# An attention block in fp32: group statistics of later images moved to VectorE, v's bias moved, last division sent through DRAM

## The chip, the cores and the metric

The kernel runs on one core of one Trainium2 chip. A core has a matrix engine (TensorE; in the profile PE for the matmuls and PEld for the weight loads), VectorE (DVE), ScalarE (ACT), GpSimd (POOL) and SyncE (SP). SP, ACT and POOL issue the DMAs here. The metric is the device time of one execution in microseconds (us). TensorE writes only to PSUM, which VectorE and ScalarE empty.

## What is computed

The input is 16 images of 512 channels by 32x32 positions (1024). Per image: group norm with 8 groups of 64 channels, a product with a 1536x512 matrix to q, k and v, attention with 4 heads of 128 channels over the 1024 positions, a product with a 512x512 matrix, and the residual. All in fp32.

```python
xg = x.reshape(b, NUM_GROUPS, -1)
mu = jnp.mean(xg, axis=-1, keepdims=True)
var = jnp.var(xg, axis=-1, keepdims=True)
xn = ((xg - mu) * jax.lax.rsqrt(var + EPS)).reshape(b, c, h, w)
xn = xn * norm_gamma[:, None, None] + norm_beta[:, None, None]
qkv = jnp.einsum('oc,bchw->bohw', qkv_w, xn) + qkv_b[:, None, None]
q, k, v = jnp.split(qkv, 3, axis=1)
...
attn = jax.nn.softmax(jnp.einsum('bhnd,bhmd->bhnm', q, k) * scale, axis=-1)
out = jnp.einsum('bhnm,bhmd->bhnd', attn, v)
out = out.transpose(0, 1, 3, 2).reshape(b, c, h, w)
out = jnp.einsum('oc,bchw->bohw', proj_w, out) + proj_b[:, None, None]
return x + out
```

## The kernel before

**Tiles.** A tile has 128 partitions. An image is 4 tiles x of 128 channels by 1024 positions; a PSUM bank holds 512 fp32 columns. An fp32 matmul appears in the profile as two instructions.

**The fast path.** The softmax is computed without subtracting a maximum. At the end one number tells whether all sums of exponentials and their inverses were in bounds (spans, LIMIT); only if not, a general path runs, which the diff touches in one line and which runs in no measurement here.

**The loop.** The main loop goes through 16 images x 4 heads x 8 steps, where a step is a block of 128 key positions. In a step `scores` (L843) makes s for both halves of the queries (L846), ScalarE takes the exponential to p (L852), VectorE adds p to the running sum tot (L858 and L860, one 128x1024 instruction a step), and one step later `weighted_sum` (L937) adds v times p to po (L942). After a head's last step ScalarE copies po to o (L949). In the next head's steps `denominators` (L864) sums tot over its partitions with transposes and a reduction on VectorE and takes the inverse r; `spread_inverse` (L887) writes r to DRAM as one row and reads the row back on all 128 partitions (rinv); `divide` (L951) multiplies o by rinv.

**What fills the steps.** Between these matmuls stand the projections, cut into units by `plan_head` (L1089). They use Strassen's seven products, for q and k, v and the output projection two levels deep (`two_levels`, L523, matmuls of 256 columns at L606; sums of the moving blocks at L574: tiles qk_t, v_t, pp_t). Their results leave PSUM at L486 and L628 (ScalarE) and L630 (VectorE), are combined at L679 and finished at L714 (q and k), L768 (v) and L826, L829 (output). While head 0 of image b runs, PE also makes q and k of b's second pair; with head 1 the output projection of b - 1; with head 2 q and k of b + 1, with head 3 v of b + 1. Weight sums are made once, during image 0 (`group_weights`, L392: tiles w, w_v, w_proj, with st_a as raw blocks), stored to DRAM (L443) and loaded again for each image through SP (L408), into buffers that two groups take in turn.

**Order.** The program is written in one order, and a scheduler orders each engine's instructions by their estimated readiness and priority. `tc.high_priority(URGENT)` brings an instruction ahead, `tc.issue_after(i)` keeps it behind instruction i, `keep_in_program_order` pins it. Each engine then runs its instructions in that fixed order, and an instruction that waits holds up what stands behind it on its engine.

**Group statistics.** During head 1 of image b, ScalarE sums each tile of image b + 1 and its squared distances (`stats_chunk`, L258, into mv: mean and variance of each channel). `stats_group` (L272) then makes 10 small steps (`Norm.group_steps`, L61): the channel means go through a matmul with a block matrix avg (pm, L83), VectorE takes the differences, their squares and adds the variances (L82 to L87), a second matmul averages these (pv, L88), VectorE adds EPS (ve, L89), GpSimd takes the power of -0.5 (rstd, L90), and sc and sh follow (L76, L100, L102). They are cut into three parts, behind tot's sums of steps 2, 3 and 4. Then ScalarE normalises x (L109). Image 0 has its own opening (`open_image`) with the same steps.

**v's bias.** Because the weights of the attention add up to 1, v's bias can be added later. `bias_of_v` (L959) multiplies it by the projection's weights, 16 small matmuls in image 0's head 1 (pb, L965), and adds the result to the projection's bias.

**The end.** The last head has no following head to hide its division. `last_division` (L898) sums tot over its partitions on PE: 8 small matmuls with a column of ones (l_last, L904), an inverse on VectorE, products with an identity, and two 512-column matmuls with a square of ones (rows, L922), which put the inverses on all partitions; VectorE multiplies o by them (L927). `last_projection` (L1023) is a one-level Strassen product (lx, ly, lz, L1031); its parts 1 and 5 need nothing of head 3, the others do. `last_span` (L930) adds the last head's check, a second matmul pair of most (L1078).

## Time and profile before

| what | value |
|---|---|
| median of 3 runs | 3172.76 us (3171.57 to 3177.14) |
| the profiled execution's span | 3170.7 us |
| VectorE busy / ScalarE / GpSimd | 83% / 45% / 16% of the span |
| granted TensorE clock | 1.00 throughout |
| one image in the steady part | about 195.8 us |
| pm (L83), 17 pairs; pv (L88), 17 pairs | first at 8 us, last at 2857 and 2864 us |
| pb (L965) | 32 instructions, 121.7 to 137.1 us |
| mean wait-free small VectorE instruction (L82 to L102) | 0.15 to 0.16 us |
| rstd (L90) on GpSimd, 128x4, median | 2.03 us |
| row to DRAM (L891), time to landing | 1.3 to 5.0 us, median 1.7 |
| rinv from DRAM (L896), 512 KB, time to landing | 3.3 to 11.1 us, median 4.9 |

Times of instructions are counted from the start of the span. A row of the order of time gives the start, the busy time, the engine, the line and operation, the tile written and the tiles read, sizes, and the number of instructions merged into the row; in brackets the idle time of the engine just before and what ended it. Matmuls overlap: their cost on PE is read from the distance between starts, not from their length.

### The profile page before, as it was taken

To read this page: it belongs to the slowest core of one execution; us is meant where nothing else is said; L and a number is where in the kernel's file an instruction comes from. 1 tells how busy PE (TensorE), PEld (TensorE's weight loads), DVE (VectorE), ACT (ScalarE), POOL (GpSimd) and SP (SyncE) were. 2 spreads that over 40 slices of the span, in tenths; PEclk is the share of its full clock that TensorE was granted. 3 is DMA by queue.
4 is the path that set the end of the run, shared out by engine and by line. 5 is a ranking of instruction groups with operands and counts; after the bars stand their busy time and mean duration, and the time that the engine had idled before them with its cause. 6 is when DMAs were issued, how large, how long until landed. Compare 5 with 4: busy or idle time off the path is not lost.

```text
span 3170.7 us, 34267 instructions
## 1 busy us (share of the span) xinstructions
PE 3159.9 (100%) x10524; PEld 2190.7 (69%) x10524; DVE 2633.6 (83%) x4639; ACT 1439.7 (45%) x2712; POOL 517.7 (16%) x898
## 2 busy tenths in 40 slices
PE   9999999999999999999999999999999999999999
PEld 7566676677766676777767767677676776766764
DVE  9878879788897888878788787987879978788784
ACT  3535435354353543545435453453534545344342
POOL 0011221111211112211122111222012221122200
PEclk9999999999999999999999999999999999999999
DMA  5554554555545455454554545555455564555531
GB/s 177 185 190 154 188 172 154 171 153 192 171 164 162 153 185 175 167 167 145 191 172 162 171 145 187 171 172 172 144 175 169 176 189 134 174 162 186 179 116 41
DMA packets 210333, 524.32 MB, mean 165 GB/s; under 512 B 32096, under 2 KB 65376, under 8 KB 210144
## 3 DMA queue, kind: packets, MB, share of 16 engines
q1 hardware_dynamic: 132896, 282.12, 28.8%
q0 software_dynamic: 64000, 204.54, 19.2%
q10 hardware_dynamic: 13248, 35.39, 3.5%
q8 instruction: 87, 1.43, 0.2%
q14 instruction: 102, 0.84, 0.1%
HBM read 388.77 MB, written 133.17 MB: 165 GB/s over the span
## 4 chain that ended last, share of the span: by engine, by line
PE 96%; DVE 3%; DMA 0%; issue 0%; POOL 0%; SPq 0%; ACT 0%; DVEq 0%; POOLq 0%
PE po L942 27%; PE s L846 27%; PE qk_x L606 12%; PE qk_y L606 9%; PE pp_x L606 6%; PE v_x L606 6%; PE pp_y L606 4%; PE v_y L606 4%; PE lx L1031 0%; DVE qk_t L574 0%; PE ly L1031 0%; PE warm L1153 0%; DVE tot L860 0%; DVE qk L714 0%; DVE qk_r L630 0%
## 5 line engine op out<-in xcount | busy, mean ns | idle before, releaser
L942 PE MATMUL po<-p,v 128*128 128x512 f32 x2048 | 1049.5, 594 | 0.7 <-ACT p L852 0.7
L846 PE MATMUL s<-qk,qk 128*128 128x512 f32 x2048 | 1047.4, 593 | 0.3 <-DVE qk L714 0.3
L852 ACT ACTIVATE p<-s 128x512 f32<-128x512 f32 x1024 | 610.9, 597 | 961.0 <-PE s L846 957.2
L942 PEld LDWEIGHTS po<-p,v 128*128 128x128 f32 x2048 | 603.6, 302 | 322.7 <-issue 214.5
L860 DVE TENSOR_TENSOR tot<-tot,p 128x1024 f32<-128x1024 f32 x385 | 469.0, 1218 | 158.4 <-ACT p L852 156.3
L846 PEld LDWEIGHTS s<-qk,qk 128*128 128x128 f32 x2048 | 387.7, 190 | 88.6 <-issue 29.9
L606 PEld LDWEIGHTS qk_x<-qk_t,w 128*128 128x128 f32 x1344 | 251.8, 190 | 166.1 <-issue 75.3
L606 PE MATMUL qk_x<-qk_t,w 128*128 128x256 f32 x1344 | 356.3, 382 | 0.1
L486 ACT COPY qk_u<-qk_x 128x512 f32<-128x512 f32 (+1 forms) x256 | 136.3, 533 | 229.2 <-PE qk_x L606 229.2
L779 POOL DMA_DIRECT2D vd<-vu x120 | 66.7, 557 | 899.8 <-DVE vu L771 897.9
L630 DVE TENSOR_TENSOR qk_r<-qk_y,qk_u 128x512 f32<-128x512 f32 (+1 forms) x256 | 157.7, 616 | 34.7 <-ACT qk_u L486 21.6
L580 POOL DMA_DIRECT2D kept_t<-qk_t x240 | 129.4, 540 | 278.4 <-DVE qk_t L574 211.9
L606 PEld LDWEIGHTS pp_x<-pp_t,w_proj 128*128 128x128 f32 x630 | 117.2, 190 | 74.7 <-issue 32.3
L784 POOL DMA_DIRECT2D v<-vd x240 | 140.6, 593 | 167.1 <-DMA vd<-vu 70.3
L630 DVE TENSOR_TENSOR v_r<-v_y,v_u 128x512 f32<-128x512 f32 (+1 forms) x120 | 76.0, 633 | 110.6 <-ACT v_u L486 80.3
L606 PE MATMUL pp_x<-pp_t,w_proj 128*128 128x256 f32 x630 | 167.8, 383 | 0.0
L606 PE MATMUL v_x<-v_t,w_v 128*128 128x256 f32 x630 | 166.6, 381 | 0.0
L830 POOL DMA_DIRECT2D out_y<-y x120 | 66.0, 550 | 604.2 <-DVE y L829 602.4
L606 PEld LDWEIGHTS v_x<-v_t,w_v 128*128 128x128 f32 x630 | 118.4, 190 | 55.3 <-issue 19.1
L606 PE MATMUL qk_y<-x,w 128*128 128x256 f32 x512 | 142.1, 379 | 0.0
L714 DVE SCALAR_TENSOR_TENSOR qk<-qk_r,qkb_sb,qk_r 128x512 f32<-128x512 f32 x192 | 137.5, 743 | 1.6
L486 ACT COPY v_u<-v_x 128x512 f32<-128x512 f32 (+1 forms) x124 | 66.3, 535 | 157.1 <-PE v_x L606 130.3
(217 smaller groups left out, 4487.2 us busy)
## 6 DMA issues: line engine op xcount, KB each, us to landing
w<-kept SPq DMA_DIRECT2D x90, 512.0 KB, 3.7
kept_t<-qk_t POOLq DMA_DIRECT2D x180, 256.0 KB, 3.3
v_t<-kept_t SPq DMA_DIRECT2D x180, 256.0 KB, 2.9
w<-kept SPq DMA_DIRECT2D x90, 384.0 KB, 3.4
rinv<-row ACTq DMA_DIRECT2D x63, 512.0 KB, 4.9
x<-in_x POOLq DMA_DIRECT2D x60, 512.0 KB, 4.6
vd<-vu POOLq DMA_DIRECT2D x120, 256.0 KB, 3.1
v<-vd POOLq DMA_DIRECT2D x240, 128.0 KB, 4.2
```

The source lines that it names most:

```text
L486: nc.scalar.copy(t[n][:, :width], t["x"][:, :width])
L580: nc.gpsimd.dma_start(t, to)
L606: nc.tensor.matmul(acc[:, ts(i, Q)], have["w"][t][:, i, slot, :], inner(i, bn), start=(first and i == 0), stop=True, skip_group_check=True,)
L630: nc.vector.tensor_add(dst, view(a), view(c))
L714: nc.vector.scalar_tensor_tensor(st[b, h][:, ts(half, HALF)], a, qkb_sb[:, i : i + 1], c, ALU.add, ALU.add)
L779: nc.gpsimd.dma_start(rows[which][ts(h, P), :], u)
L784: nc.gpsimd.dma_start(vs[b, pair][ts(q, BLK), half].rearrange("m h (k i) j -> m (h k) (i j)", k=n), rows[which].rearrange("(k m) (q e) -> ...
L830: nc.gpsimd.dma_start(out[b, ts(o, P), ts(half, HALF)], t)
L846: nc.tensor.matmul(sc, ks[b, h][:, ts(j, P)], qs[b, h][:, ts(half, HALF)], start=True, stop=True)
L852: exps[s] = nc.scalar.activation(ps[s][:, ts(half, HALF)], sc, AF.Exp, scale=SCALE)
L860: added[b, h, j] = nc.vector.tensor_add(tot[b, h][:, i], tot[b, h][:, i], ps[s][:, i])
L942: nc.tensor.matmul(po[b, h][:, i], v_block(b, h, j), ps[s][:, i], start=(j == 0), stop=(j == NB - 1),)
```

## The change

- The statistics of images 1 to 15 make no matmul. ScalarE writes means and sums of squared distances into one table of 128 x 2 x 32, of which 4 columns each are used and the rest is zero. VectorE transposes the table by blocks of 32x32, copies each block of 32 partitions beside its partner, so that the 64 channels of a group stand in one row with a count of 1024 each, and aggregates them with the instruction that combines means and spreads (bn_aggr). It adds EPS; GpSimd takes the power on one column; VectorE transposes mean and power back and makes sc and sh. All of it is one unit, behind tot's sum of step 3, urgent. Image 0 keeps its old way.
- v's bias is added to v where v is finished (images 1 to 15, with the addition at L768 as a three-operand instruction), and to image 0's attention output on ScalarE after its division. `bias_of_v` is gone.
- The last head's denominators go the way of the others: `denominators` on VectorE, urgent, r to DRAM through SP, and the row back on all partitions in two halves through SP and ACT; VectorE multiplies each half. ones_sq, the identity, the small matmuls and `last_span` are gone; spans has one more column. In `last_projection` the first chunks of products 2 and 6, which need nothing of head 3, come ahead of their second chunks.

```diff
@@ -256,41 +256,54 @@
     norm = Norm(nc, gn, ps_a, avg, neghalf, gamma_sb, beta_sb, NCC, N, "y")
 
     def stats_chunk(b, c):
-        if c == 0:
-            mvs[b] = gn.tile([P, NCC, 2], F32, tag="mv", name=f"mv_{b}")
-
+        mean, spread_ = (
+            (mvs[b][:, c, 0:1], mvs[b][:, c, 1:2]) if b == 0
+            else (table[:, 0, c : c + 1], table[:, 1, c : c + 1])
+        )
         junk = lpool.tile([P, N], F32, tag="tt", name=f"junk_{b}_{c}")
         sums = gn.tile([P, 3], F32, tag="st", name=f"sums_{b}_{c}")
         nc.scalar.activation(junk, xs[b, c], AF.Identity, accum_out=sums[:, 0:1])
-        nc.scalar.mul(mvs[b][:, c, 0:1], sums[:, 0:1], 1.0 / N)
+        nc.scalar.mul(mean, sums[:, 0:1], 1.0 / N)
         nc.scalar.mul(sums[:, 1:2], sums[:, 0:1], -1.0 / N)
         nc.scalar.activation(
-            junk, xs[b, c], AF.Square, bias=sums[:, 1:2], accum_out=sums[:, 2:3]
+            junk, xs[b, c], AF.Square, bias=sums[:, 1:2],
+            accum_out=sums[:, 2:3] if b == 0 else spread_,
         )
-        nc.scalar.mul(mvs[b][:, c, 1:2], sums[:, 2:3], 1.0 / N)
+        if b == 0:
+            nc.scalar.mul(spread_, sums[:, 2:3], 1.0 / N)
 
     def stats_group(b):
 
 
-        g = []
-
-        def part(n, first, last):
-            if not g:
-                g.extend(norm.group_steps(mvs[b]))
-            with tc.issue_after(added[b - 1, 1, n].ins), tc.high_priority(URGENT):
-                for step in g[first:last]:
-                    step()
-
-        def scale():
-            n = 4 if b > 1 else 3
-            part(n, 9, 10)
-            with tc.issue_after(added[b - 1, 1, n].ins), tc.high_priority(URGENT):
-                mu, sc = norm.result
-                sh = norm.shift(mu, sc)
+        v = nc.vector
+        quads = P // BLK
+        k = slice(0, NCC)
+
+        def steps():
+            t = lpool.tile([P, N], F32, tag="tt", name=f"groups_{b}")
+            rows = t[:, : 6 * BLK].rearrange("p (s j) -> p s j", s=3)
+            both = t[:, 6 * BLK : 6 * BLK + 2]
+            ve = t[:, 6 * BLK + 2 : 6 * BLK + 3]
+            back = t[:, 8 * BLK : 10 * BLK].rearrange("p (s j) -> p s j", s=2)
+            v.memset(rows[:, 0, :], float(N))
+            v.transpose(rows[:, 1:3, :BLK], table)
+            for q in range(quads):
+                v.tensor_copy(rows[ts(q, BLK), 1:3, BLK:], rows[ts(q ^ 1, BLK), 1:3, :BLK])
+            v.bn_aggr(both, rows.rearrange("p s j -> p j s"))
+            v.tensor_scalar_add(ve, both[:, 1:2], EPS)
+            nc.gpsimd.tensor_tensor(both[:, 1:2], ve, neghalf[:, 0:1], ALU.pow)
+            v.transpose(back, both.unsqueeze(2).to_broadcast([P, 2, BLK]))
+            sc = gn.tile([P, NCC], F32, tag="sc", name="sc")
+            v.tensor_mul(sc, back[:, 1, k], gamma_sb)
+            sh = norm.shift(back[:, 0, k], sc)
             for c in range(NCC):
                 scaled[b, c] = sc, sh, c
 
-        return [lambda: part(2, 0, 6), lambda: part(3, 6, 9), scale]
+        def all_():
+            with tc.issue_after(added[b - 1, 1, 3].ins), tc.high_priority(URGENT):
+                steps()
+
+        return all_
 
     def normalise(b, c, half, on_scalar=True):
         t = xs[b, c][:, ts(half, HALF)]
@@ -765,7 +778,8 @@
                 )
             n = P // BLK
             t = ypool.tile([P, HALF], F32, tag="y", name=f"vt_{b}_{pair}_{h}_{half}")
-            nc.vector.tensor_add(t, a, c)
+            i = 2 * pair + h
+            nc.vector.scalar_tensor_tensor(t, a, vb_sb[:, i : i + 1], c, ALU.add, ALU.add)
 
             u = ypool.tile([P, HALF], F32, tag="y", name=f"vu_{b}_{pair}_{h}_{half}")
             nc.vector.transpose(
@@ -896,43 +910,15 @@
         nc.scalar.dma_start(rinv[b, h], rows_of.pop((b, h)).to_broadcast((P, N)))
 
     def last_division(b, h):
-
-
-        t = tot.pop((b, h))
-        acc = ps_s.tile([P, HALF], F32, tag="s", name="l_last")
-        for j in range(NB):
-            nc.tensor.matmul(
-                acc[:, j : j + 1], t[:, ts(j, P)], ones_sq[:, 0:1], start=(j == 0), stop=True,
-                skip_group_check=True,
-            )
-        r = lpool.tile([P, NB], F32, tag="part", name="r_last")
-        nc.vector.reciprocal(r, acc[:, :NB])
-        l = lpool.tile([P, NB], F32, tag="l", name="l_col")
-        nc.scalar.copy(l, acc[:, :NB])
-        blocks = lpool.tile([P, NB, P], F32, tag="tt", name="r_blocks")
-        n = NB // NH2
+        row = dpool.tile([1, N], F32, tag="row", name="row_last")
+        inv = lpool.tile([P, N], F32, tag="rinv", name="rinv_last")
+        nc.sync.dma_start(row.rearrange("o (c i) -> (o c) i", i=BLK), inverse.pop((b, h)))
+        for half, eng in enumerate((nc.sync, nc.scalar)):
+            i = ts(half, HALF)
+            eng.dma_start(inv[:, i], row[:, i].to_broadcast((P, HALF)))
         for half in range(NH2):
-            i = ts(half, n)
-            nc.vector.tensor_mul(
-                blocks[:, i, :], late["ident"].unsqueeze(1).to_broadcast([P, n, P]),
-                r[:, i].unsqueeze(2).to_broadcast([P, n, P]),
-            )
-        for half in range(NH2):
-            rows = ps_s.tile([P, HALF], F32, tag="s", name=f"rows_{half}")
-            nc.tensor.matmul(
-                rows, ones_sq, blocks[:, ts(half, n), :].rearrange("p j q -> p (j q)"),
-                start=True, stop=True,
-            )
             i = ts(half, HALF)
-            nc.vector.tensor_mul(os_[b, h][:, i], os_[b, h][:, i], rows)
-        return l, r
-
-    def last_span(l, r):
-        worst = lpool.tile([P, NB], F32, tag="worst", name="worst_last")
-        span = gn.tile([P, 1], F32, tag="span", name="span_last")
-        nc.vector.tensor_max(worst, l, r)
-        nc.vector.tensor_reduce(span, worst, AX.X, ALU.add)
-        return span
+            nc.vector.tensor_mul(os_[b, h][:, i], os_[b, h][:, i], inv[:, i])
 
     def weighted_sum(s, half):
         b, h, j = where(s)
@@ -950,25 +936,15 @@
 
     def divide(b, h):
         nc.vector.tensor_mul(os_[b, h], os_[b, h], rinv.pop((b, h)))
+        if b == 0:
+            nc.scalar.activation(
+                os_[b, h], os_[b, h], AF.Identity, bias=vb_sb[:, h : h + 1]
+            )
 
     def spread(plan, units, first, last):
 
         for i, u in enumerate(units):
             plan[first + i * (last - first) // len(units)].append(u)
-
-    def bias_of_v(o):
-
-        acc = ps_a.tile([P, HALF], F32, tag="y", name=f"pb_{o}")
-        half, r = divmod(o, 2)
-        for c in range(NCC):
-            block = stage["proj"][f"a{half + 1}{c // KC + 1}"]
-            nc.tensor.matmul(
-                acc[:, 0:1], block[:, ts(r * KC + c % KC, P)], vb_sb[:, c : c + 1],
-                start=(c == 0), stop=(c == NCC - 1),
-            )
-        nc.vector.tensor_add(
-            projb_sb[:, o : o + 1], projb_sb[:, o : o + 1], acc[:, 0:1]
-        )
 
     def kept_group(site, g):
         if g == 0:
@@ -1026,8 +1000,8 @@
         y, bl = late["y"], ob[b]
         x_, y_, z_, kept_ = {}, {}, {}, {}
 
-        def mm(acc, r, p, first):
-            for k in range(KC):
+        def mm(acc, r, p, first, ks=range(KC)):
+            for k in ks:
                 nc.tensor.matmul(
                     acc, late["w"][p][:, ds((r * KC + k) * P, P)], bl[FACTORS[p][1]][k],
                     start=(first and k == 0), stop=(k == KC - 1), skip_group_check=True,
@@ -1049,7 +1023,7 @@
             x_[r] = ps_a.tile([P, HALF], F32, tag="x", name=f"lx_{r}")
             mm(x_[r], r, 1, True)
             copy(r, "p1")
-        l, recip = last_division(b, HEADS - 1)
+        last_division(b, HEADS - 1)
         sums_of_b(bl, (2, 3), (1,))
         for r in range(2):
             y_[r] = ps_a.tile([P, HALF], F32, tag="y", name=f"ly_{r}")
@@ -1057,15 +1031,18 @@
             add(0, r, 0, kept_["p1", r], False)
         for r in range(2):
             z_[r] = ps_s.tile([P, HALF], F32, tag="s", name=f"lz_{r}")
-            mm(z_[r], r, 2, True)
+            mm(z_[r], r, 2, True, (0,))
+        for r in range(2):
+            mm(x_[r], r, 6, False, (0,))
+        for r in range(2):
+            mm(z_[r], r, 2, True, (1,))
             add(0, r, 0, z_[r], True)
         for r in range(2):
-            mm(x_[r], r, 6, False)
+            mm(x_[r], r, 6, False, (1,))
             copy(r, "u2")
         for r in range(2):
             add(0, r, 1, kept_["u2", r], False)
 
-        span = last_span(l, recip)
         total = gn.tile([BLK, 1], F32, tag="total", name="total")
         nc.vector.tensor_reduce(total, spans, AX.X, ALU.add)
         for r in range(2):
@@ -1074,8 +1051,7 @@
             add(1, r, 1, kept_["u3", r], False)
             add(1, r, 1, y_[r], True)
         most = ps_s.tile([P, HALF], F32, tag="s", name="most")
-        nc.tensor.matmul(most[:1, :1], total, ones, start=True, stop=False)
-        nc.tensor.matmul(most[:1, :1], span, ones_sq[:, 0:1], start=False, stop=True)
+        nc.tensor.matmul(most[:1, :1], total, ones, start=True, stop=True)
         ok = gn.tile([1, 1], F32, tag="fine", name="fine")
         nc.vector.tensor_scalar(ok, most[:1, :1], LIMIT, None, ALU.is_le)
         fine.append(ok)
@@ -1104,14 +1080,7 @@
             else:
                 plan[0].append(lambda: load_x(b + 1))
                 spread(plan, [lambda c=c: stats_chunk(b + 1, c) for c in range(NCC)], 2, 4)
-                sums, power, scale = stats_group(b + 1)
-                if b == 0:
-
-                    plan[4] += [sums, power, scale]
-                else:
-                    plan[4].insert(0, sums)
-                    plan[4].insert((len(plan[4]) + 1) // 2, power)
-                    plan[5].insert(0, scale)
+                plan[4].insert(0, stats_group(b + 1))
                 for r in range(2):
                     plan[5 + r] += [
 
@@ -1124,7 +1093,6 @@
                     plan[g // 2].append(lambda g=g: kept_group("v", g))
                     plan[NB // 2 - 1 + g].append(lambda g=g: kept_group("proj", g))
                 plan[2].append(lambda: stage_blocks("proj"))
-                spread(plan, [lambda o=o: bias_of_v(o) for o in range(NCC)], 3, 5)
         elif b + 1 == B:
             if h == 2:
                 plan[0].append(lambda: last_loads("w"))
@@ -1268,6 +1236,8 @@
         if s > 0:
             del ps[s - 1]
 
+    with tc.high_priority(URGENT):
+        denominators(B - 1, HEADS - 1)
     last_projection(B - 1)
     nc.vector.tensor_scalar(flag, fine[0], -1.0, 1.0, ALU.mult, ALU.add)
 
@@ -1354,7 +1324,9 @@
                         acc[:, :P], vs[j][:, ts(h, P)], pT[:, j, :],
                         start=(j == 0), stop=(j == NB - 1),
                     )
-                nc.scalar.copy(o[h][:, ts(qb, P)], acc[:, :P])
+                nc.scalar.activation(
+                    o[h][:, ts(qb, P)], acc[:, :P], AF.Identity, bias=vb_sb[:, h : h + 1]
+                )
         for i in range(NCC):
             for half in range(NH2):
                 acc = product(lambda c: wproj[c][:, ts(i, P)], lambda c: o[c][:, ts(half, HALF)])
```

Left out of this diff are only the declarations (spans, table, the zeroing of table on GpSimd, ones_sq) and the identity in `last_loads`.

## What is predicted, and from what

> **What bounds the kernel now.** I read the page's busy times and its chain first, then the order of time around the group statistics of a late image, then the same for image 0 and for the end, then single groups for prices.
>
> From the page, busy time, then the chain that ended last by engine:
> ```profile
> PE 3159.9 (100%) x10524; PEld 2190.7 (69%) x10524; DVE 2633.6 (83%) x4639; ACT 1439.7 (45%) x2712; POOL 517.7 (16%) x898
> ...
> PE 96%; DVE 3%; DMA 0%; issue 0%; POOL 0%; SPq 0%; ACT 0%; DVEq 0%; POOLq 0%
> ```
> TensorE (PE) is never idle and is 96% of the chain. A busy PE need not be a full one, so I checked its starts. Order of time, image 14's head 1 (statistics of image 15), PE alone:
> ```profile
> 2856.21 1.03 PE L606 MATMUL pp_x<-pp_t,w_proj 128*128 128x256 f32 x4
> 2857.07 0.28 PE L83 MATMUL pm<-mean,avg 128*128 128x4 f32 x2
> 2857.22 1.11 PE L606 MATMUL pp_x<-ot,w_proj 128*128 128x256 f32 x4
> 2858.16 1.02 PE L846 MATMUL s<-qk,qk 128*128 128x512 f32 x2
> ...
> 2863.34 0.59 PE L606 MATMUL pp_y<-o,w_proj 128*128 128x256 f32 x2
> 2863.77 0.59 PE L606 MATMUL pp_y<-ot,w_proj 128*128 128x256 f32 x2
> 2864.28 0.39 PE L88 MATMUL pv<-vv,avg 128*128 128x4 f32 x2
> 2864.53 1.10 PE L846 MATMUL s<-qk,qk 128*128 128x512 f32 x2
> 2865.47 1.02 PE L942 MATMUL po<-p,v 128*128 128x512 f32 x2
> ```
> Groups follow each other by count alone: four of 256 columns take 0.86 us (2856.21 to 2857.07), two of 512 also 0.86 (2858.16 to the next group at 2859.02). Every PE instruction taken out here shortens the kernel, as long as what feeds PE keeps up.
>
> The Trainium skill (Trainium Kernel Development and Optimization, section Performance Expectations) warns that matmul busy time says little and weight-load busy time more. By that rule 69% would leave PE room, VectorE (DVE, 83%) would be nearest to the bound, and a change that loads it would gain nothing; the even starts speak against it here. Its mechanism is rival 1.
>
> **Images 2 to 15: two small matmuls less.** pm: from its start to s is 1.09, of which four L606 are 0.86: 0.23 us. pv: the two L606 at 2863.77 would have made room at 2864.20; po follows at 2865.47 after s's 0.86: 0.41 us, of which some 0.08 is pv's wait for its bank. 0.64 x 14 images = **9.0 us saved**, if nothing new makes PE wait.
>
> What VectorE gets in exchange, per image. Rows: memset 128x4 0.06 and 128x128 0.17, so 0.10; a transpose of 128x64 between 0.20 (32x32) and 1.23 (128x1024), near the small one, 0.25, twice; four 32x64 copies at 0.20 (32x32 adds 0.18); the sum with EPS and three small products and differences at 0.15. The aggregate over 192 elements has no row: 12 elements took 0.21; at the rate of the 512-element statistics (0.68) it is 0.35, and at the 12-element row's excess over a 0.15 small instruction (5 ns an element) 1.1; I take 0.45, since the other streaming rows follow the first rate. Sum 2.45, bounds 1.6 (small ones overlapping, as d and mu below 0.1 us apart) and 3.1.
>
> The four copies each start in another group of 32 partitions. Such rows (L874, then L875, 3110.86 to 3111.06) start 0.20 apart, while d and mu on the same partitions started 0.07 apart. The Trainium skill (VectorE: DVE Perf Modes, section Two Vector instructions with no wait between them) says that an instruction whose start quadrant changes is held until all earlier ones finished; by that rule the copies cost 0.8, without it 0.3, and the rows agree with the rule.
>
> Where this lands: all steps wait for tot's third sum, which is the one at 2859.85 (it ends 2861.08). Order of time, VectorE:
> ```profile
> 2860.99 0.76 DVE L574 TENSOR_TENSOR pp_t<-ot,pp_t 128x256 f32<-128x256 f32 x2
> 2861.66 0.68 DVE L829 TENSOR_TENSOR y<-y,pp_r 128x512 f32<-128x512 f32 x1
> 2863.54 0.69 DVE L630 TENSOR_TENSOR pp_r<-pp_y,pp_p 128x512 f32<-128x512 f32 x1 [1.19 <-PE pp_y L606]
> 2864.40 0.69 DVE L630 TENSOR_TENSOR pp_r<-pp_y,pp_u 128x512 f32<-128x512 f32 x1 [0.17 <-PE pp_y L606]
> ...
> 2886.44 0.75 DVE L574 TENSOR_TENSOR qk_t<-x,qk_t 128x256 f32<-128x256 f32 x2
> ...
> 2889.25 1.03 PE L606 MATMUL qk_x<-qk_t,w 128*128 128x256 f32 x4
> ```
> The new work fills 1.36 us of idle time (1.19 + 0.17), and ve, sc, t and sh leave (0.34 by start to start). What is left, 2.45 - 1.36 - 0.34 = 0.75 us, makes VectorE late, and from 2865 to 2912 it has almost no gap (26.00 of 27 us busy from 2885 to 2912). Late next would be qk_t's sums, behind tot's last sum. They end at 2887.19, PE reads them at 2889.25: 2.06 us of cover, less the 0.64 that PE is now ahead, 1.42. 0.75 fits in, the upper bound (1.40) just so: **stall 0**, with no more than some tenths per image as the doubt. The pp_t sums behind the new steps at 2861 are read by PE at 2866.3, four us later. The power on GpSimd shrinks from 4 columns to 1 (2.03 us median before); it starts earlier, and the y loads of L813 queued behind its wait go earlier with it; sc and sh, so the ScalarE normalising behind them (2871.3), too. ScalarE loses one 0.2 us multiply per chunk, covered either way. The bound if the scheduler leaves VectorE waiting for the power is in rival 1.
>
> **v's bias.** 120 additions (0.70) become three-operand ones (0.74, L714): 8 x 0.05 per image in the v stretch, where VectorE has gaps of 1 to 4 us. **Nothing.** Four extra 128x1024 passes on ScalarE for image 0 (1.05 each, by the statistics' row), ScalarE being 45% busy, and their reader waits until head 0 of image 1, step 6: nothing; uncovered they would be 4 us. The memset of the table on GpSimd precedes gamma's load, which lands some 4 us before its reader at 10 us: nothing.
>
> **Image 0, where the PE work goes but not the time.** PE loses pb's 32 instructions and pm and pv, with waits: from 122.18 to 124.82 less s's 0.86 is 1.78; from 130.83 to 133.38 less 0.86 is 1.69 (1.2 of it a wait for mean); from 134.24 to 138.15 less s and po 2.19. Sum 5.66. But the chain in order of time has no PE there; it runs through VectorE's weight sums, a store and a load:
> ```profile
> 149.42 0.20 DVE w_proj L440
> 149.65 4.04 DMA kept_proj<-w_proj
> 153.71 5.40 DMA w<-kept
> 159.24 1.97 PE qk_x L606 x8
> ```
> PE already waited 1 us for that load at 159.24; it would arrive 5.7 us sooner and wait 5.7 longer. VectorE's part of this chain gets 2.45 more, and loses nine small instructions and two bias sums (0.9 start to start) and an idle 0.93 before sc: **+0.7 us**. Bounds: -5.2 if the chain shortens almost as PE does, +3.0 if two sums of tot (1.14 each) are pulled in ahead.
>
> **The end.** l_last's 16 instructions cost 1.70 to ly's start and 0.08 behind; rows' four 1.72; the second of the most pairs 0.12: **3.6 us saved**. In exchange the division goes the long way: tot ends 3135.64; head 2's denominators ran from 3108.33 to r's end at 3112.06, 3.73, so r at 3139.40; row's DMA 1.7 (median; 1.3 to 5.0); half of rinv as the 256 KB transfers of that stretch, 2.8; a product 0.69: 3144.6. PE by then: lx to 3140.34, ly 3.43, then four instructions each for lz's and lx's first chunk, 3.43: 3147.20. Cover 2.6 us: no stall. What it costs uncovered: rival 3.
>
> **Sum.** -9.0 + 0.7 - 3.6 = -11.9 us against the profiled span of 3170.7: 3158.8. The median of the runs is 2.06 above that span, so 3172.76 - 11.9 = **3160.9 us**, 0.38% faster. Its own range: 3157 to 3165.
>
> **Rivals.**
> 1. Slower: VectorE takes over from 2861 to 2912. If it also stands through the power (2.03) with nothing placed in between and the aggregate costs 1.1, it is 3.1 + 2.0 - 0.34 - 1.36 = 3.4 late against a cover of 1.42: 2.0 us of PE wait in 14 images, 28 us, 3189. It decides from 2.27 late on (0.85 per image eats the 11.9). For: VectorE's gapless 26.00 of 27 us; against: sc before the change stood behind other work and never waited in later images.
> 2. A smaller lateness, 1.8: 0.4 per image, 5.6 back, 3166.5. For: bounds reach 1.4 late by the aggregate alone.
> 3. The division's DMAs are slow: 5.0 and 11.1, their longest: product at 3156.2, 9 us of PE wait, 3169.9. Against: those times are from stretches full of transfers, the end has almost none (41 GB/s in the last slice).
> 4. Image 0 goes to its upper bound, 3.0: 3163.2.
>
> **Chances.** Forecast 0.60, rival 1 0.10, rival 2 0.15, rival 3 0.05, rival 4 0.10. A measurement tells 0.2% (6.3 us) from no change; faster means below 3166.4. The forecast, rival 4 and 0.06 of rival 2: 0.76; same 0.14 (rival 3 and the rest of 2); slower 0.10. Range 3155 (image 0's lower bound) to 3171 (rival 3); rival 1 and some of the rest lie outside.
>
> **What would show it.** PE without L83 and L88 in later images and its groups still 0.86 apart around 2850 to 2900, period 0.64 shorter; qk_x<-qk_t without a wait for VectorE; in image 0 a PE wait of 6 to 7 us for w<-kept; at the end lz's second chunk without a wait. Wrong if L606 shows waits for VectorE once per image, if the aggregate takes over 1.1 us, or if PE waits for os_ at the end.

## The result and the profile after

The changed kernel takes 3177.45 us (median of 19 runs, 3176.20 to 3179.85) against 3172.55 us (19 runs, 3170.65 to 3177.14) for the kernel before: a ratio of 1.0016, 95% interval 1.0010 to 1.0022. It was forecast 0.4% faster and is 0.15% slower; by the 0.2% bound of the prediction that is no change, though the interval leaves out 1. In 12 of the 19 runs of the changed kernel the mean granted clock was 0.999 (median 3178.57 us) and in 7 it was 1.000 (3176.61 us), while the kernel before shows 0.999 in only 3 of its 22 runs beside e1, so about 1 us of the difference may lie there. The profiled span went from 3170.7 to 3174.6 us at the same clock (1.0).

From the page of the changed kernel, busy time and the chain by engine, the two lines that the prediction began with:
```profile
PE 3151.4 (99%) x10410; PEld 2178.7 (69%) x10410; DVE 2658.4 (84%) x4683; ACT 1439.1 (45%) x2655; POOL 496.2 (16%) x897
...
PE 68%; issue 23%; DVE 7%; POOL 1%; DMA 0%; SPq 0%; POOLq 0%; ACT 0%; DVEq 0%
```
TensorE has 114 instructions and 8.5 us of busy time less, and still the span is 3.9 us longer: it now stands idle some 12 us more than it did, 9.5 of them in images 1 to 14.

Where that is, the starts of the scores show. The first scores matmul of an image, in us from the start of the span:

| start of | before | after | after less before |
|---|---|---|---|
| image 1 | 240.49 | 239.23 | -1.26 |
| image 2 | 436.28 | 435.70 | -0.58 |
| image 8 | 1611.12 | 1614.08 | +2.96 |
| image 14 | 2785.87 | 2792.39 | +6.52 |
| the last scores matmul | 3133.69 | 3140.80 | +7.11 |
| the last PE instruction | 3164.44 | 3167.95 | +3.51 |

Image 0 gave 1.3 us, the end gave 3.6 and took 0.4 back behind its last matmul. The steady images, where 0.64 us each was to be won, lose 0.59 each (from image 2 to 14: 2356.69 us against 2349.59, over 12). So one thing has to be explained: a swing of 1.23 us per image. All but the 0.13 us of v's operand (e3 below) lies in head 1, steps 4 and 5, once in each image.

TensorE there, order of time of the changed kernel, image 9's head 1 (columns: start, busy, engine, line and operation, tiles, sizes, rows merged; in brackets idle before and its releaser):
```profile
1893.73 1.03 PE L619 MATMUL pp_x<-pp_t,w_proj 128*128 128x256 f32 x4
1894.59 1.02 PE L860 MATMUL s<-qk,qk 128*128 128x512 f32 x2
1895.45 1.02 PE L928 MATMUL po<-p,v 128*128 128x512 f32 x2
1896.91 1.13 PE L619 MATMUL pp_x<-pp_t,w_proj 128*128 128x256 f32 x4 [0.44 <-ACT pp_u L499]
1898.28 1.13 PE L619 MATMUL pp_y<-ot,w_proj 128*128 128x256 f32 x4 [0.24 <-DVE pp_r L643]
```
From start to start it is 1.46 and 1.37 us where 0.86 is full speed: 1.11 us, and the step behind the second wait takes 0.96, another 0.10. The kernel before loses 0.09 at this place (pp_x to po, 2871.49 to 2872.44, image 14). The waits are the same in every image from 1 to 14. The first wait is for ScalarE's copy of the bank into pp_u, the second for VectorE's sum pp_r, which must have read the bank before pp_y may write it again. The same rows of ScalarE and of VectorE:
```profile
1892.98 1.52 ACT L109 ACTIVATE x<-x,sh,sc 128x512 f32<-128x512 f32 x2 [1.04 <-DVE sh L102]
1894.40 0.57 ACT L866 ACTIVATE p<-s 128x512 f32<-128x512 f32 x1
1894.88 1.50 ACT L109 ACTIVATE x<-x,sh,sc 128x512 f32<-128x512 f32 x2
1896.29 0.56 ACT L499 COPY pp_u<-pp_x 128x512 f32<-128x512 f32 x1
```
```profile
1884.22 1.23 DVE L874 TENSOR_TENSOR tot<-tot,p 128x1024 f32<-128x1024 f32 x1 [0.83 <-ACT p L866]
...
1885.94 0.78 DVE L291 COPY groups<-groups 32x64 f32<-32x64 f32 x4
1886.75 0.42 DVE L587 TENSOR_TENSOR pp_t<-ot,pp_t 128x256 f32<-128x256 f32 x1
1887.10 1.01 DVE L292 BATCH_NORM_AGGREGATE groups<-groups 128x2 f32<-128x192 f32 x1
...
1888.57 0.14 DVE L293 TENSOR_SCALAR groups<-groups 128x1 f32<-128x1 f32 x1
1888.63 0.68 DVE L643 TENSOR_TENSOR pp_r<-pp_y,pp_p 128x512 f32<-128x512 f32 x1
1890.11 0.24 DVE L295 STREAM_TRANSPOSE groups<-groups 128x64 f32<-128x64 f32 x1 [0.80 <-POOL groups L294]
...
1897.54 0.68 DVE L643 TENSOR_TENSOR pp_r<-pp_y,pp_u 128x512 f32<-128x512 f32 x1
```
Three things can be read here. On ScalarE four halves of the normalising and an exponential stand ahead of pp_u, although the bank that it copies was full at about 1894.8; the kernel before has this copy first. On VectorE the group statistics run as the diff has them, and then VectorE stands 0.80 us for the power on GpSimd. And pp_r comes 13.32 us after the start of tot's third sum; in the kernel before it is 11.64 (2859.85 to 2871.49, image 14). ScalarE and VectorE there:
```profile
2870.83 0.59 ACT L486 COPY pp_u<-pp_x 128x512 f32<-128x512 f32 x1 [1.12 <-PE pp_x L606]
2871.31 0.82 ACT L109 ACTIVATE x<-x,sh,sc 128x512 f32<-128x512 f32 x1
...
2859.85 1.23 DVE L860 TENSOR_TENSOR tot<-tot,p 128x1024 f32<-128x1024 f32 x1 [0.60 <-ACT p L852]
```

### The profile page after: what moved, and what is told of

Its sections match the earlier page's. It is cut to its first block, busy times and chain, and to the rows that moved or that the text cites. A ratio compares the mean times of both kernels' runs of the same rounds, so it can differ in the third digit from the quotient of the medians.

```text
span 3174.6 us, 33990 instructions
## 1 busy us (share of the span) xinstructions
PE 3151.4 (99%) x10410; PEld 2178.7 (69%) x10410; DVE 2658.4 (84%) x4683; ACT 1439.1 (45%) x2655; POOL 496.2 (16%) x897
## 3 DMA queue, kind: packets, MB, share of 16 engines
q8 instruction: 86, 1.41, 0.2%
## 4 chain that ended last, share of the span: by engine, by line
PE 68%; issue 23%; DVE 7%; POOL 1%; DMA 0%; SPq 0%; POOLq 0%; ACT 0%; DVEq 0%
PE po L928 19%; PE s L860 19%; PE qk_x L619 9%; PE qk_y L619 7%; PE v_x L619 6%; PE v_y L619 4%; PE pp_y L619 1%; PE pp_x L619 1%; DVE pp_r L692 1%; DVE o L938 1%; DVE qk_t L587 1%; DVE pp_r L643 1%; DVE qk_r L643 0%; DVE tot L874 0%; POOL x L235 0%
## 5 line engine op out<-in xcount | busy, mean ns | idle before, releaser
L785 DVE STREAM_TRANSPOSE vu<-vt 128x512 f32<-128x512 f32 x120 | 136.0, 1133 | 2.1 <-DMA vd<-vu 2.1
```

The costliest lines, as they stand in the source:

```text
L785: nc.vector.transpose(u.rearrange("p (q i j) -> p j q i", q=n, i=BLK), t.rearrange("p (j q i) -> p j q i", q=n, i=BLK),)
```

## The experiments

Two theories at first. A: scale and shift come earlier in VectorE's order, so the normalising moved ahead of pp_u in ScalarE's fixed order, and that is the wait. B: VectorE's added work makes pp_r late. Later a third, C, that TensorE's own order moved too.

Each run was timed beside the kernel before on the same chip. "Period" is the mean length of images 2 to 13 against the kernel before (0.00), from the starts of image 2 and image 14 in the profile.

**Scale and shift later (e1).** The statistics stay on VectorE, cut in two: the part up to the power behind tot's third sum, the rest behind the fourth.
```diff
+        return [lambda: part(3, steps), lambda: part(4 if b > 1 else 3, scale)]
...
-                plan[4].insert(0, stats_group(b + 1))
+                first_, second_ = stats_group(b + 1)
+                plan[4].insert(0, first_)
...
+                    plan[5].insert(0, second_)
```


> The changed kernel with its unit cut in two: transposing back, sc, t and sh stand behind tot's sum of step 4 again, as before the change; all instructions are the same. Theory A (ScalarE's queue): TensorE's wait of 0.60 + 0.40 us per image at pp_x and pp_y, with the 0.1 behind each, comes from the normalising put ahead of the copy pp_u in ScalarE's fixed order; here the copy stands first, the wait goes, 14 x 1.2 = 17 us less: span about 3158, time about 3160. Theory B (VectorE's added 2 to 3 us of work per image makes it late): the work is all there, the wait stays within 0.3 us per image: time 3173 to 3177.

3166.93 us (10 runs), ratio 0.9984 (0.9975 to 0.9994); period -0.12. So 0.71 of the 1.23 us an image goes with where the second half stands. VectorE in this kernel no longer stands for the power, since other sums lie between the halves:
```profile
1888.98 1.22 DVE L880 TENSOR_TENSOR tot<-tot,p 128x1024 f32<-128x1024 f32 x1
1890.12 0.24 DVE L301 STREAM_TRANSPOSE groups<-groups 128x64 f32<-128x64 f32 x1
...
1893.73 0.68 DVE L649 TENSOR_TENSOR pp_r<-pp_y,pp_u 128x512 f32<-128x512 f32 x1
```
pp_r is 12.22 us behind tot's third sum (1881.51). TensorE's order is that of the kernel before again, apart from pm and pv. This edit changes two engines' orders and VectorE's wait at once, so it can't tell A from B.

**The normalising behind the kept copies (e2).** A alone: only the normalising of ScalarE is held back.
```diff
+    def gated_normalise(b, c, half, on_scalar):
...
+        with tc.issue_after(last_copy[-1].ins):
+            return normalise(b, c, half, on_scalar)
```


> The changed kernel with only ScalarE's normalising held behind the last copy of a TensorE product made so far; VectorE's statistics unit is as in the change. Theory A: the wait at pp_x goes (14 x 1.2 us), time 3160 to 3163. Theory B: VectorE is as loaded and as early as in the change, the wait stays, time 3173 to 3177.

3186.54 us, ratio 1.0045 (1.0028 to 1.0062); period +1.26. It went the other way. TensorE, the same place:
```profile
1902.10 1.11 PE L627 MATMUL pp_x<-pp_t,w_proj 128*128 128x256 f32 x4
1904.66 1.13 PE L627 MATMUL pp_y<-ot,w_proj 128*128 128x256 f32 x4 [1.45 <-DVE pp_r L651]
1905.63 1.03 PE L936 MATMUL po<-p,v 128*128 128x512 f32 x2
```
The wait for pp_u is gone, as A has it, but the one for pp_r grew from 0.24 to 1.45. A is not enough. The third row matters as well, but I only saw that later: po's weighted sums stand behind pp_y here, so the edit moved TensorE's order too, and it is not A alone.

**A plain add at v (e3).** v's bias is left out of v for images 1 to 15, by the two-operand add of the kernel before.
```diff
-            nc.vector.scalar_tensor_tensor(t, a, vb_sb[:, i : i + 1], c, ALU.add, ALU.add)
+            nc.vector.tensor_add(t, a, c)
```


> The changed kernel with v's bias left out for images 1 to 15 (the addition at v is a two-operand one again). Theory: the three-operand addition is 0.05 us longer and stands before the sums that free a bank for v_y; TensorE's wait there grew from 0.09 to 0.24 us per image: 15 x 0.15 = 2.3 us less than the changed kernel, 3175. Rival (the v stretch has cover, the 0.15 comes from elsewhere): no change, 3177.5.

3175.59 us, ratio 1.0012 (1.0002 to 1.0021), 1.9 us less than the changed kernel; period +0.46 against +0.59. The medians alone don't separate the two kernels (their runs overlap), but the place does: TensorE's step from po to v_y in head 3 takes 0.56 to 0.58 us in images 1 to 13 of the changed kernel and is even, 0.43, in e3. The third operand costs 0.13 us an image, where "nothing" was forecast.

**The kernel before with its scale early (e4).** No added work on VectorE; scale and shift of the kernel before are put behind tot's third sum instead of the fourth.
```diff
-            n = 4 if b > 1 else 3
+            n = 3
...
-                    plan[5].insert(0, scale)
+                    plan[4].insert((len(plan[4]) + 1) // 2 + 1, scale)
```


> The kernel before, with its matmul statistics, but sc and sh behind tot's sum of step 3 instead of step 4, so that ScalarE's normalising may be placed earlier; no work is added anywhere. Theory A: normalising moves ahead of pp_u in ScalarE's order, TensorE waits 0.3 to 1.2 us per image there, 4 to 17 us more than before: 3177 to 3190. Theory B: no added work, no wait: 3172 to 3173.

3181.82 us, ratio 1.0029 (1.0018 to 1.0041); period +0.66. Giving the normalising its operands sooner costs the kernel before nearly 10 us by itself. So the early scale is a cause without any new VectorE work. It is not quite the wait of the changed kernel: po again stands ahead of the second pp_x, but only two halves of the normalising stand ahead of pp_u, and that step costs 0.18 us. More is lost at the next group's pp_x, 0.39 from start to start, where ScalarE's copy pp_p stands behind further halves:
```profile
1904.31 0.70 PE L606 MATMUL pp_x<-pp_t,w_proj 128*128 128x256 f32 x2 [0.23 <-ACT pp_p L486]
```

**The later scale with v's bias as before (e5).** e1, with the plain add at v, pb's 16 matmuls back in image 0 and no ScalarE pass over its outputs.
```diff
-            nc.vector.scalar_tensor_tensor(t, a, vb_sb[:, i : i + 1], c, ALU.add, ALU.add)
+            nc.vector.tensor_add(t, a, c)
...
+                spread(plan, [lambda o=o: bias_of_v(o) for o in range(NCC)], 3, 5)
```


> The version of the run that cut the statistics in two (transposing back, scale and shift behind the 4th running sum), with v's bias treated as before: a plain add at v, pb's 16 matmuls back in image 0 and no ScalarE pass over its attention outputs. Theory (v's added operand costs VectorE's late stretch 0.13 to 0.16 us an image; image 0 is set by the w<-kept load either way): 14 x 0.13 = 1.8 less than 3166.9, and 0 to 2 for pb's matmuls: 3165 to 3167, about 6 below the kernel before. Rival (with the stretch no longer late, v's operand is hidden, and pb's matmuls cost their 5.7 us on TensorE): 3170 to 3172, no better than before.

3166.49 us (11 runs), ratio 0.9984 (0.9975 to 0.9993); period -0.26, again 0.14 less than with the operand. The medians of e1 and e5 lie 0.4 us apart, which their ranges don't separate. Image 1 starts at 240.65 with pb and at 240.49 in the kernel before: pb's matmuls bring back no 5.7 us.

**The end alone (e6).** The kernel before with the new last division and last_projection, nothing else.

> The kernel before with only the new end: the last division through the two transfers, last_projection with its reordered sums, no span_last; statistics and v's bias as before. Theory (the end is worth 3.6 us by itself, less 0.4 in the last tail): span 3167.5, time 3169 to 3169.5, ratio 0.9989. Rival (the 3.6 us came from something that the other parts shifted ahead of it, such as the load of w or VectorE's order): 3171 to 3173, not told from before.

3169.16 us (11 runs), ratio 0.9991 (0.9982 to 1.0000); last PE instruction 3.43 us earlier, span 3.0 us shorter. The end is worth what was expected, apart from the rest of the change.

**The copies first, without the power (e7).** e2 with the power left out for images 1 to 15.
```diff
-            v.tensor_scalar_add(ve, both[:, 1:2], EPS)
-            nc.gpsimd.tensor_tensor(both[:, 1:2], ve, neghalf[:, 0:1], ALU.pow)
+            v.tensor_scalar_add(both[:, 1:2], both[:, 1:2], EPS)
```


> The version that keeps ScalarE's kept copies ahead of the normalising (3186.5; TensorE waits 1.45 us an image for VectorE's pp_r), with one thing more: for images 1 to 15 the power on GpSimd is left out, so these images are normalised by the variance plus epsilon and not by its inverse root. VectorE then has no 0.80 us wait between the add of epsilon and the transposing back, which was 1.40 us from end to start. Theory B (that wait stands in VectorE's own stream and makes everything behind it late): pp_r comes 0.8 to 1.3 us earlier, TensorE's wait falls from 1.6 to 0.3 to 0.8 us an image, time 3186.5 - 14 x 0.8 to 1.3 = 3168 to 3175. Rival (VectorE is held by the running sums, which come when the exponentials do, so that the 0.8 us only turn up again as other idle time): wait and time stay, 3184 to 3187.

3180.11 us, ratio 1.0026 (1.0015 to 1.0036); period +0.82. That is 6.4 us less than e2, 0.43 an image: some half of what B expected. pp_r comes 12.62 us behind tot's third sum here (1886.72 to 1899.34) and 13.05 in e2 (1890.87 to 1903.92). The wait of 0.80 is gone, but the small steps that hang on one another now follow without other work in between, and take 0.80 us from start to start (1891.08 to 1891.61, 1892.21 to 1892.48) instead of 0.51. And TensorE still waits 1.02 us, though pp_r is only 0.98 later than in the kernel before. That points to TensorE's order: in the kernel before po's weighted sums stand between pp_x and pp_y, in e2 and e7 behind pp_y, in the changed kernel ahead of the second pp_x.

**No bias pass in image 0 (e8).** The four ScalarE passes that add v's bias to image 0's attention output are left out.

> The changed kernel without ScalarE's pass that adds v's bias to image 0's four attention outputs (the bias of image 0 is left out, nothing else). Theory (these passes make TensorE wait 1.35, 0.99 and 0.77 us in image 0's heads, but image 0 ends with the wait for the w<-kept load): the three waits go, the wait for w<-kept grows by as much, time 3175 to 3178, not told from the changed kernel. Rival (the passes cost their waits outright): 3177.5 - 3.1 = 3174.4 or less, with image 1 starting 3 us earlier.

3177.43 us, level with the changed kernel. The time is what the theory gave, but the waits did not go. In the changed kernel and then in this one, TensorE's rows with a wait, from image 0's head 1 to the reader of w<-kept:
```profile
133.77 1.12 PE L860 MATMUL s<-qk,qk 128*128 128x512 f32 x2 [1.35 <-ACT p L866]
140.17 1.13 PE L860 MATMUL s<-qk,qk 128*128 128x512 f32 x2 [0.99 <-ACT p L866]
142.06 1.12 PE L860 MATMUL s<-qk,qk 128*128 128x512 f32 x2 [0.77 <-ACT p L866]
157.76 0.67 PE L619 MATMUL qk_x<-x,w 128*128 128x256 f32 x2 [1.43 <-DMA w<-kept]
```
```profile
140.18 1.24 PE L860 MATMUL s<-qk,qk 128*128 128x512 f32 x2 [2.45 <-ACT p L866]
142.07 2.07 PE L860 MATMUL s<-qk,qk 128*128 128x512 f32 x2 [0.65 <-ACT p L866]
```
3.11 us against 3.10. The bias pass stood ahead of the first of these exponentials in the changed kernel, but taking it out shortens nothing: the first wait joins the second, since the exponentials stand behind a normalising that waits for sh (it starts at 138.12 in the changed kernel, after 2.60 us of idle time that sh ended, and at 138.13 here, after 4.06).

That no wait for w<-kept shows in the second kernel is not the edit's doing. In its profiled execution the granted clock was 0.5 from 141.06 to 147.89 us, where the changed kernel's shows 1.0, and TensorE came to the reader of that load at 158.96 us, after it had landed (157.89). So the two profiles can't be compared behind this place, and whether the load would hide what the passes cost stays open.

**Both orders as before (e9).** e2, and pp_y of the third group is issued one half of a step later, so that po goes first.
```diff
+                if b > 0:
+                    p7, p4, p3, *normals = plan[5]
+                    plan[5] = [p7, p4] + 3 * [lambda: None] + [p3] + normals
```


> The version that keeps ScalarE's kept copies ahead of the normalising (3186.5), with one thing more: in images 1 to 14 the third group's last product in step 5, pp_y, is issued one half later, so that TensorE runs the two weighted-sum matmuls ahead of it, as the kernel before does and as the changed kernel and that version don't. ScalarE's order stays. VectorE gets two 0.42 us sums pp_t ahead of pp_r, which the kernel before has there too. Theory C (the changed kernel lost 0.86 us of cover because TensorE's own order moved as well): TensorE's wait for pp_r falls from 1.61 us an image by 0.86, less 0.68 if the two sums stand in front of pp_r, to 0.75 to 1.4; time 3186.5 - 14 x 0.2 to 0.86 = 3174.5 to 3184. With both orders as before, what is left over the version cut in two (3166.9) is VectorE alone. Rival (VectorE's lateness only moves on and TensorE waits the same total one product later): 3186 to 3187.

3174.54 us, ratio 1.0009 (0.9999 to 1.0018), 12.0 us less than e2; period +0.39. TensorE:
```profile
1894.26 1.11 PE L627 MATMUL pp_x<-pp_t,w_proj 128*128 128x256 f32 x4
1895.21 1.03 PE L936 MATMUL po<-p,v 128*128 128x512 f32 x2
1896.82 1.13 PE L627 MATMUL pp_y<-ot,w_proj 128*128 128x256 f32 x4 [0.57 <-DVE pp_r L651]
```
pp_r is as late as in e2 (13.05 behind the third sum), and the wait is 0.88 shorter: that much cover was TensorE's own order, as C has it. What is left, 0.57, is VectorE alone: its statistics as in the changed kernel, the two other engines up to this place in the order of before.

**Both orders as before, without the power (e10).** The edits of e9 and e7 together.

> The version with ScalarE's kept copies ahead of the normalising and TensorE's weighted sums ahead of pp_y (3174.5; TensorE still waits 0.57 us an image for pp_r), with the power on GpSimd left out for images 1 to 15 (they are normalised by the variance plus epsilon). Theory B (what is left is VectorE, and of it 0.80 us is its own wait for the power): a 0.69 us sum of blocks moves ahead of pp_r and a 0.42 us pp_t behind it, so pp_r comes 0.5 us earlier and the wait of 0.57 all but goes: 3174.5 - 14 x 0.5 = 3167.5, level with the version cut in two. Rival (the wait is filled by other work as soon as it goes, pp_r comes no earlier): 3174 to 3175.

3182.57 us, ratio 1.0031 (1.0019 to 1.0043); period +0.89. A miss, by 15 us. At its place the edit did about what was expected: pp_r comes 12.62 behind the third sum, and the step to pp_y shrank by 0.43 us. But a new wait stands at the next group's pp_y, and VectorE shows why (its rows stand below TensorE's):
```profile
1911.93 1.04 PE L934 MATMUL po<-p,v 128*128 128x512 f32 x2
1913.64 0.70 PE L625 MATMUL pp_y<-o,w_proj 128*128 128x256 f32 x2 [0.67 <-DVE pp_r L649]
...
1912.04 1.22 DVE L880 TENSOR_TENSOR tot<-tot,p 128x1024 f32<-128x1024 f32 x1
1913.18 0.41 DVE L649 TENSOR_TENSOR pp_r<-pp_y,pp_u 128x256 f32<-128x256 f32 x1
```
In e9 this pp_r stands ahead of the running sum (1906.54 and 1907.47), here behind it. With sh earlier the order of VectorE's own sums changed once more. Neither theory has the net result; it shows that a shorter way to sh can be paid back by the order that it brings.

**The division later (e11).** e5, with one piece of VectorE's work taken out of the stretch, and pp_y issued one half of a step later, so that TensorE keeps the order of the kernel before.
```diff
-                if half == 1 and j == 4 and s > NB:
+                late_ = 6 if h == 1 and b > 0 else 4
+                if half == 1 and j == late_ and s > NB:
...
+                    scale, p7, p4, p3, *normals = plan[5]
+                    plan[5] = [scale, p7, p4] + 2 * [lambda: None] + [p3] + normals
```


> The version cut in two with v's bias as before (3166.5), with one piece of VectorE's work moved: in head 1 of images 1 to 15 the division of the head before by its denominators, 1.22 us and 1.13 from start to start, stands behind the 6th running sum instead of the 4th; pp_y is issued one half later, so that TensorE's order stays as it was. Theory (VectorE has no gap from the statistics to pp_r, so what is taken out ahead of pp_r comes off its lateness): a 0.69 us sum moves ahead and a 0.42 us one too, pp_r comes 0.2 to 0.5 us earlier, TensorE's wait of 0.20 and the 0.1 of its restart go: 3166.5 - 14 x 0.2 to 0.3 = 3162.3 to 3163.7. Rival (the division comes too late for something behind it, or the wait has another releaser): 3166 or more.

3162.23 us (7 runs, 3161.95 to 3163.08), ratio 0.9970 (0.9958 to 0.9981): faster than both kernels, and just outside the expected range on the fast side. Period -0.57, against the 0.64 that pm and pv were to give. TensorE goes through without a wait at this place (image 9):
```profile
1887.88 1.11 PE L625 MATMUL pp_x<-pp_t,w_proj 128*128 128x256 f32 x4
1888.83 1.03 PE L933 MATMUL po<-p,v 128*128 128x512 f32 x2
1889.70 1.03 PE L625 MATMUL pp_y<-ot,w_proj 128*128 128x256 f32 x4
1890.57 1.02 PE L865 MATMUL s<-qk,qk 128*128 128x512 f32 x2
```

## Why the prediction was wrong, step by step

**pm and pv, 9.0 us: right as a price.** It shows only where the waits are gone: in e11 eight of the twelve images are 0.61 to 0.65 us shorter than before. The mean of -0.57 is short of 0.64 through image 4, where pp_y of a later group waits 0.34 us for its pp_r, and images 10 and 11, where that pp_y comes late by 0.1 to 0.3 (v's bias is as before in e11, so its 0.14 is not in it).

**"Stall 0" in images 2 to 15: wrong, and nearly the whole error.** The profiled span missed its forecast by 15.8 us (3174.6 against 3158.8): images 1 to 15 are 17.4 worse than forecast, with v's operand in that, the end behind TensorE's last instruction 0.4 worse, image 0 2.0 better. The stall of 0 rested on three parts.

*How late VectorE is.* Forecast 0.75 us. The added work itself was well priced: from start to start in the changed kernel 2.36 us (memset 0.02, transposing 0.11, copies 0.81, aggregate 0.93, EPS 0.06, transposing back 0.17, sc, t and sh 0.26) against 2.45. The aggregate was twice its 0.45: it follows the upper of the two rates that the prediction had from rows, 5 ns an element, and not the one it chose. The small instructions were cheaper. The four copies took 0.78, 0.2 each; that agrees with the rule of the Trainium skill (VectorE: DVE Perf Modes, section Two Vector instructions with no wait between them) that a change of start quadrant holds an instruction. What was wrong is the idle time: it was to be filled by 1.36 us, but 0.80 of it came back as VectorE's own wait for the power, so only 0.56 was filled. 2.36 - 0.34 - 0.56 = 1.46 us late; measured in e9, where the two other engines are in the order of before, 13.05 - 11.64 = 1.41. That is the first half of rival 1, which had the wait for the power.

*What is late next.* The prediction took qk_t's sums, with 1.42 us of cover. It passed over the reader before them. TensorE and VectorE in the kernel before, image 14:
```profile
2871.49 1.11 PE L606 MATMUL pp_x<-pp_t,w_proj 128*128 128x256 f32 x4
2872.44 1.04 PE L942 MATMUL po<-p,v 128*128 128x512 f32 x2
2873.31 1.03 PE L606 MATMUL pp_y<-ot,w_proj 128*128 128x256 f32 x4
...
2871.49 0.68 DVE L630 TENSOR_TENSOR pp_r<-pp_y,pp_u 128x512 f32<-128x512 f32 x1
```
pp_r ends at 2872.17, pp_y starts at 2873.31: 1.14 us, less the 0.41 of pv, which stood in between and goes, leaves 0.73. 1.41 against 0.73 makes a wait of 0.68; e9 shows 0.57 idle, 0.75 from start to start. These rows were in the profile of before. A sum that frees a bank is a reader's condition as much as one that makes an operand, and it was not looked for.

*The orders.* "sc and sh, so the ScalarE normalising behind them (2871.3), too" go earlier, the prediction says, as if that cost nothing. It cost ScalarE's order (the wait for pp_u) and TensorE's (po moved). There was no cover for that: in the kernel before the copy pp_u ends at 2871.42 and pp_x starts at 2871.49. e4 shows an earlier scale alone in the kernel before, with both orders moved: 9.5 us. Against e9 the changed kernel's own mix of orders costs another 0.20 us an image, 2.9 us by the medians; e2 shows that putting back ScalarE's order alone can cost more than leaving both, because TensorE's order then moves once more.

So the period goes from -0.57 (no wait, e11) to +0.39 by VectorE's lateness with the v operand (e9) and +0.59 by the orders on top (after).

**Rival 1** named the right engine and half of the mechanism, with a time too high (3189): VectorE does stand for the power, but the wait ends at pp_y, not at qk_t, and is 1.1 us an image, not 2.0, in part through ScalarE. The rule of the Trainium skill that the prediction set aside (Trainium Kernel Development and Optimization, section Performance Expectations) is not what decided: e11 has VectorE at 84%, as the changed kernel has, and TensorE's even starts back.

**v's bias, "nothing":** mis-sized. 0.13 us an image (e3) and 0.14 (e5 against e1), nearly 2 us in all.

**Image 0, +0.7:** -1.3 in the profile, inside its bounds, but not by the forecast's steps. VectorE's part of the chain did not grow (the store of w_proj begins at 149.39, before at 149.65), and the store and the load took 4.77 and 3.45 us, before 4.04 and 5.40: 1.2 us less together, which no step of the forecast had. So that it fell inside the bounds is in good part luck. pb's matmuls bring nothing there that stands out of the spread, as forecast (e5). Of the wait of 6 to 7 us for w<-kept only 1.43 came; 3.1 us went to ScalarE's exponentials instead.

One profile does not settle image 0's share. Image 1 starts at 239.23 in the changed kernel and at 243.14 in e3, whose edit bears on v of images 1 to 15 alone. Of these 3.9 us, 2.35 are there when TensorE has the load (157.76 and 160.11); the rest goes with a granted clock of 0.5 from 160.64 to 164.06 us in e3's profile. The profiles of e1, e2, e3, e8 and e10 have such a stretch in image 0, the others don't.

**The end, -3.6: right.** From lx's first start to the last PE instruction it is 25.00 us, 28.60 before. The last division's product did not make TensorE wait:
```profile
3152.60 1.88 PE L1005 MATMUL lx<-ot,wl 128*128 128x512 f32 x4
3154.31 1.88 PE L1005 MATMUL lz<-o,wl 128*128 128x512 f32 x4
3156.03 1.88 PE L1005 MATMUL lx<-ot,wl 128*128 128x512 f32 x4
3157.84 0.18 PE L1054 MATMUL most<-ones,total 32*1 32x1 f32 x2
```
1.71 and 1.72 from start to start, four full ones each. The cover was half of the forecast, though: VectorE ends the product at 3152.98 and TensorE's reader starts at 3154.31, 1.3 us against 2.6; the two halves of the row took 3.7 and 3.9 us to land, where 2.8 was taken. The stretch behind the last PE instruction grew by 0.4 us, which no step had.

**Open:** why the scheduler's ordering of each engine's instructions comes out as it does for a given position of sc and sh was not looked into; only the orders and their price were seen. Nor was it looked into why the granted clock falls in image 0 of some executions.

## What to carry to other kernels

When work is added to an engine with a gapless stretch, list every instruction of the bound engine in that stretch with what it needs, banks to be freed included, and compare the lateness with the smallest cover, not with the one that looks most like a dependency. A result that becomes ready earlier can move its users ahead of urgent work on engines with a fixed order; look at the order on all engines before the price of any instruction. Split a step that goes through another engine and put other work between the halves, and move what has slack out of the stretch: that, with v's bias left as it was, turned a loss of 4.9 us into a gain of 10.

## What the runs showed of the hardware that was not expected

The aggregate of batch-norm statistics over 192 elements took 1.01 us on VectorE, 5.3 ns an element, where the streaming rows of the same engine had 1.2 to 1.3 (a 128x1024 sum takes 1.22 us, a 128x512 one 0.68).

A power of one column on GpSimd took 0.56 us, but it was 1.40 us from the end of VectorE's addition (1888.71) to the start of the transposing back, 0.80 of it idle. GpSimd issued a store of y first, which took 0.55:
```profile
1888.95 0.55 POOL L844 DMA_DIRECT2D out_y<-y  x1 [28.75 <-DVE groups L293]
1889.51 0.56 POOL L294 TENSOR_TENSOR groups<-groups,neghalf 128x1 f32<-128x1 f32 x1
```
A wait of TensorE costs more than the idle time that the profile lists: the first step of 256 columns behind it is 0.32 us instead of 0.22 (rows of four take 1.13 behind a wait, 1.03 elsewhere as a rule, and 1.11 at some places where no wait is listed). In 14 images with two waits each that is 2.9 us of the changed kernel's loss.

In image 0 of five profiles, between 141 and 164 us, the granted clock falls to 0.5 for 3.4 us (6.8 in e8) and comes back to 1.0. In e8 TensorE's instructions of 512 columns then start 0.85 us apart instead of 0.43.
